# Cross attention over 16 batches: the narrow product before the projection and the queries, the tokens' product before the small ones, Wout loaded in batch 1, another order in the last batch

## The chip, the cores and the metric

The kernel runs on one core of a Trainium2 chip. The metric is the device time of one execution in microseconds, lower is better. All data are float32.

## The reference

For each of 16 batches there are 100 rows of hidden states `x` (640 wide) and 722 context rows (384 wide), of which the last 4 are the tokens `ca` and the first 718 are `enc`. With 8 heads of 80:

```python
query, keyt, valt = x @ Wq, enc @ Wk, enc @ Wv
hs = mha(query, keyt, valt)                          # 100 queries, 718 keys
ca_q1 = einsum('btc,th->bch', ca, Wq_ca)[:, indices] # 100 of 384 rows
ca_hs1 = mha(ca_q1, x, x)                            # 100 queries, 100 keys
ca_hs2 = mha(ca_hs1 @ Wq, ca @ Wk_ca, ca @ Wv_ca)    # 100 queries, 4 keys
out = (hs + ca_hs2) @ Wout + b_out + x
```

`mha` scales by 1/sqrt(80), takes a softmax over the keys and multiplies with the values.

## The kernel before

Everything is laid out once and then one loop runs over the batches `b`. Inside the loop the order of instructions on each engine is the order of the program text (the loop stands under a manual schedule). Tiles come from pools with a fixed number of buffers, and an instruction that writes a tile waits for the last reader of the buffer's former tile. PSUM has three pools of two buffers: `ps2` (pairs of banks), `psk` and `ps1` (single banks).

One turn of the loop does, on TensorE (PE) in this order, with the names that the profile shows:

- `s_ps` (L643), the scores of batch b in three groups, 32 contraction rows at a time in four row groups of the array. ScalarE (ACT) copies them to `st`, VectorE (DVE) takes their running maximum `most`.
- `z_ps` (L842, `softmax2`), 32 small products of the first token softmax `e1` with `y`, in column groups of 32.
- `y_ps` (L780, `second.products`), the tokens' product of batch b + 1: ten matmul passes over the whole array. GpSimd (POOL) makes the first token scores of batch b + 1 from it (`scores1`), which wait for DVE's maximum.
- `v_psA` to `v_psE` (L468) and `k_psA` to `k_psE` (L499), the values of batch b and the keys of batch b + 1, in 15 blocks each after a fast matrix multiplication plan; each block's result is added into `vs` or `kT` by DVE or copied by ACT (L439, L441). `vv.go(n)` and `kk.go(n)` issue the next n blocks; between them stand the steps of the softmax: `top.go` (the maximum over keys, turned with DVE transposes), `subtract(i)` and `exponential(i)` on `st`, and the second token softmax (`scores2`, `softmax3`). `softmax3` ends with `p2t` on DVE, which goes through DRAM (`p_d`, `wide_d`) into `pb`, from which POOL makes `hs2` (`values2`, L918 and L922).
- `kT_ps` (L593), the last chunk of the keys of batch b + 1.
- `o_ps` (L1037, `last.project`), the output projection of a row block of 128 rows that is complete. Row blocks do not line up with batches; it runs in batches 2, 3, 4, 6, 7, 8, 10, 11, 12, 14 and 15. DVE adds it to `xn` (x plus bias), and SyncE (SP) stores it.
- `q_ps` (L569, `queries`), the queries of two batches, in odd batches up to 13.
- `r_ps` (L1385), the narrow product: sums of exponentials and the last 16 values of each head, in column groups of 32. `mine.divide` follows: ACT and DVE invert the sums, SP spreads them through DRAM into `ratio`, and ACT and DVE write the last chunk of `hsT`.
- `a_ps` (L1403), the wide product: the other 64 values of each head, in column groups of 64. `keep` copies it to `hsT`, and `place` on POOL scales it by `ratio` and adds `hs2`.

`wout_sb`, the projection's weights, lies where a weight of the start-up was, and is loaded by ten DMAs that POOL issues in batch 0 (`load_outputs`, L84 and L90).

Batch 15 has no next batch: no `y_ps`, no keys, no queries. It projects 64 rows early (`project_few`, L1065), a block of 128 rows between `r_ps` and `a_ps`, and the last 128 rows after `a_ps`; there `finish` on DVE does what `keep` and `place` do elsewhere.

Of the kernel before, what the change touches and what calls it, by code (L numbers as in the profile page):

```python
# [10 lines left out]
ALU = mybir.AluOpType  # L11
# [142 lines left out]
def kernel(  # L154
# [779 lines left out]
    class Last:  # L934


        def __init__(self, b):
            self.b = b
            self.split = b == B - 1
# [87 lines left out]
        def project(self, chunks=(HC - 1, *range(HC - 1))):  # L1027
            for r, xn in self.xn.items():
                lo, n = OC[r]
                if self.split:  # L1030
                    self.o_ps = [bank(f"o_ps_{r}_{k}") for k in range(2)]
                else:
                    self.o_both = pair(f"o_ps_{r}")
                    self.o_ps = [self.o_both[:, k] for k in range(2)]
                o_ps = self.o_ps
                for c, k in [(c, k) for k in range(2) for c in chunks]:
                    nc.tensor.matmul(  # L1037
                        o_ps[k][:n, : H // 2],
                        hsTs[r][:, c, :n],
                        wout_sb[:, c, k * (H // 2) : (k + 1) * (H // 2)],  # L1040
                        start=(c == chunks[0]),
                        stop=(c == chunks[-1]),
                    )
                o_v = out.rearrange("b s n -> (b s) n")[lo : lo + n]
                if self.split:
                    for k in range(2):
                        cols = slice(k * (H // 2), (k + 1) * (H // 2))
                        nc.vector.tensor_tensor(
                            xn[:n, cols], o_ps[k][:n, : H // 2], xn[:n, cols], ALU.add
                        )  # L1050
                        nc.sync.dma_start(out=o_v[:, cols], in_=xn[:n, cols])
                    continue
                both = xn[:n].rearrange("p (k d) -> p k d", k=2)
                nc.vector.tensor_tensor(
                    both, self.o_both[:n, :, : H // 2], both, ALU.add
                )
                nc.sync.dma_start(out=o_v, in_=xn[:n])
# [155 lines left out]
    for b in range(B):  # L1213
# [5 lines left out]
        def loads():  # L1219

            if b == 0:
                load_outputs(nc.gpsimd.dma_start, wout_sb, wout)
            if b + 2 >= B:
                return None, None
            x_next = xT_at[0] if b % 2 else load_x(p + 1)
            xT_at[0] = x_next
            return Second(b + 2, x_next), load_enc(b + 2)
# [33 lines left out]
        now.softmax2()  # L1261
        if b + 1 < B:
            second.products()
            second.copy()
        seen = larger(2)
# [34 lines left out]
        elif b + 1 < B:  # L1300
# [8 lines left out]
            if b + 2 < B:  # L1309
                m_next = load_m(b + 2)  # L1310
                keys(m_next)
            top.go(3)
# [34 lines left out]
            last.project()  # L1347
        else:
# [5 lines left out]
            last.project_few(len(OC) - 2)  # L1354
            now.scores2()
# [66 lines left out]
    last.project()  # L1422
# [50 lines left out]
```

## Time and profile before

| | |
|---|---|
| timed runs | 941.51, 944.74, 940.45 us; median 941.51 |
| the profiled execution | 942.46 us, its span 940.5 us |
| granted TensorE clock, mean | 0.999 |
| PE busy | 925.5 us, 98% |
| DVE, POOL, ACT busy | 659.0 (70%), 600.7 (64%), 377.4 us (40%) |
| DMA, mean | 74 GB/s |
| share of the chain that ended last | PE 91%, DVE 4%, DMA 2%, issue 1%, POOL 1% |

PE, DVE, ACT and POOL are the engines; PEld is the loading of PE's weights, which overlaps PE. SPq, POOLq and ACTq are the queues that issue DMAs. A float32 matmul shows as two passes, so five matmuls are x10. In the timeline a row is a run of like instructions: start, length from the first start to the modelled end of the last, and then engine, line, operation, out<-in and tile (rows * columns of the array). In the chain of waits the pieces do not overlap, and "issue" is time in which an engine waited for nothing that the profile shows. A row of the waits gives the total, the number of times and the longest. A row of the windows gives the stretch, its length, then busy time and instructions of PE, PEld, DVE, ACT and POOL, the granted clock, the DMA engines' mean busy share and GB/s.

### The profile page before, as it was taken

To read this page: it belongs to the slowest core of one execution; us is meant where nothing else is said; L and a number is where in the kernel's file an instruction comes from. 1 tells how busy PE (TensorE), PEld (TensorE's weight loads), DVE (VectorE), ACT (ScalarE), POOL (GpSimd) and SP (SyncE) were. 2 spreads that over 40 slices of the span, in tenths; PEclk is the share of its full clock that TensorE was granted. 3 is DMA by queue.
4 is the path that set the end of the run, shared out by engine and by line. 5 is a ranking of instruction groups with operands and counts; after the bars stand their busy time and mean duration, and the time that the engine had idled before them with its cause. 6 is when DMAs were issued, how large, how long until landed. Compare 5 with 4: busy or idle time off the path is not lost.

```text
span 940.5 us, 26015 instructions
## 1 busy us (share of the span) xinstructions
PE 925.5 (98%) x11183; PEld 784.4 (83%) x11183; DVE 659.0 (70%) x1102; ACT 377.4 (40%) x649; POOL 600.7 (64%) x616
## 2 busy tenths in 40 slices
PE   9999999999999999999999999999999999999997
PEld 6998879788797888988788888988889788897855
DVE  3359794977929678495955959488692977849592
ACT  1235444434334344543425434344432434443340
POOL 5848699667466774658674575775756668564543
PEclk9999999999999999999999999999999999999999
DMA  8613523051410404132131412205141050402202
GB/s 266 200 39 74 141 64 86 1 144 29 107 43 11 140 9 108 29 87 86 28 94 29 119 40 60 70 8 143 30 108 42 2 144 14 107 26 54 61 23 76
DMA packets 68267, 69.16 MB, mean 74 GB/s; under 512 B 26040, under 2 KB 62072, under 8 KB 68152
## 3 DMA queue, kind: packets, MB, share of 16 engines
q1 hardware_dynamic: 66280, 64.54, 25.7%
q0 software_dynamic: 1008, 1.98, 1.0%
q8 instruction: 88, 1.44, 0.6%
q10 hardware_dynamic: 864, 0.98, 0.3%
q14 instruction: 27, 0.22, 0.1%
HBM read 61.81 MB, written 8.94 MB: 75 GB/s over the span
## 4 chain that ended last, share of the span: by engine, by line
PE 91%; DVE 4%; DMA 2%; issue 1%; POOL 1%; ACT 1%; POOLq 0%; SPq 0%; ACTq 0%; DVEq 0%
PE s_ps L643 12%; PE v_psA L468 10%; PE v_psB L468 8%; PE kT_ps L593 8%; PE k_psA L499 7%; PE q_ps L569 7%; PE a_ps L1403 7%; PE o_ps L1037 6%; PE k_psB L499 6%; PE r_ps L1385 4%; PE v_psC L468 3%; PE k_psC L499 3%; PE y_ps L780 2%; PE v_psD L468 2%; PE v_psE L468 1%; PE v_ps L409 1%
## 5 line engine op out<-in xcount | busy, mean ns | idle before, releaser
L918 POOL TENSOR_TENSOR hs<-pb,vaT 128x500 f32<-128x500 f32 x64 | 79.9, 1258 | 164.7 <-DMA pb<-wide_d 162.2
L815 POOL TENSOR_TENSOR e<-ca,g 100x800 f32<-100x800 f32 x64 | 100.7, 1584 | 68.4 <-DVE most L1245 58.4
L468 PE MATMUL v_psA<-wv_sb,enc 128*120 128x320 f32 x352 | 109.8, 435 | 0.7 <-DVE vs L439 0.6
L534 POOL TENSOR_TENSOR enc<-enc 128x240 f32<-128x240 f32 x135 | 94.2, 708 | 16.9 <-PE q_ps L569 9.8
L643 PE MATMUL s_ps<-qp,kT 32*120 32x100 f32 x3072 | 100.3, 263 | 2.5 <-issue 2.4
L643 PEld LDWEIGHTS s_ps<-qp,kT 32*120 32x120 f32 x3072 | 96.7, 180 | 5.5 <-issue 3.5
L822 POOL TENSOR_TENSOR e<-e,e 100x800 f32<-100x800 f32 x48 | 93.5, 1947 | 3.8
L468 PE MATMUL v_psB<-wv_sb,enc 128*120 128x320 f32 x296 | 91.9, 433 | 0.9 <-DVE vs L439 0.9
L1256 DVE TENSOR_TENSOR most<-st 120x800 f32<-120x800 f32 x16 | 19.5, 1220 | 99.5 <-ACT st L671 99.5
L499 PE MATMUL k_psA<-enc,wk_sb 128*128 128x240 f32 x360 | 87.7, 367 | 0.0
L1245 DVE TENSOR_TENSOR most<-most,st 120x800 f32<-120x800 f32 x64 | 70.6, 1102 | 23.2 <-ACT st L665 22.1
L1233 DVE TENSOR_TENSOR st<-st,over 120x1600 f32<-120x1600 f32 x47 | 86.0, 1830 | 0.0
L468 PEld LDWEIGHTS v_psA<-wv_sb,enc 128*120 128x120 f32 x352 | 63.2, 183 | 23.8 <-DVE vs L439 1.6
L499 PEld LDWEIGHTS k_psA<-enc,wk_sb 128*128 128x128 f32 x360 | 68.4, 190 | 16.6 <-POOL enc L534 0.2
L1241 ACT ACTIVATE st<-st 120x1600 f32<-120x1600 f32 x48 | 73.7, 1538 | 18.8 <-DVE st L1233 17.8
L468 PEld LDWEIGHTS v_psB<-wv_sb,enc 128*120 128x120 f32 x296 | 54.2, 183 | 22.9 <-DVE vs L439 1.4
L499 PE MATMUL k_psB<-enc,wk_sb 128*128 128x240 f32 x300 | 73.0, 366 | 0.0
L922 POOL TENSOR_TENSOR hs<-hs,hs 128x500 f32<-128x500 f32 x48 | 68.4, 1426 | 3.8
L1403 PE MATMUL a_ps<-st,vs 120*64 120x100 f32 (+1 forms) x1536 | 69.5, 250 | 0.0
L569 PE MATMUL q_ps<-xT,wq_sb 128*128 128x200 f32 x400 | 69.1, 333 | 0.0
L1403 PEld LDWEIGHTS a_ps<-st,vs 120*64 120x64 f32 (+1 forms) x1536 | 66.4, 137 | 2.7 <-issue 2.6
L569 PEld LDWEIGHTS q_ps<-xT,wq_sb 128*128 128x128 f32 x400 | 67.9, 190 | 0.6
(167 smaller groups left out, 1830.2 us busy)
## 6 DMA issues: line engine op xcount, KB each, us to landing
pb<-p_d SPq DMA_DIRECT2D x32, 400.0 KB
enc<-in_enct SPq DMA_DIRECT2D x30, 240.0 KB
enc<-in_enct SPq DMA_DIRECT2D x15, 360.0 KB
xT<-in_xt SPq DMA_DIRECT2D x8, 500.0 KB
rest<-in_enct SPq DMA_DIRECT2D x31, 120.0 KB
xn<-in_x SPq DMA_DIRECT2D x11, 320.0 KB
out<-xn SPq DMA_DIRECT2D x11, 320.0 KB
wide_d<-p_d SPq DMA_DIRECT2D x16, 200.0 KB
```

Of the source, the lines that this page charges most:

```text
L468: nc.tensor.matmul(at[0][j][:KN, : H // 2], a_form(self.enc, f)[:, j * KN : (j + 1) * KN], wv_there.get(f, wv_sb[:, W_AT[f]]), start=first ...
L499: nc.tensor.matmul(at[:, i * KT : (i + 1) * KT], wk_sb[:, W_AT[f], i], a_form(self.enc, f), start=(first and i == 0), stop=last, skip_grou ...
L534: nc.gpsimd.tensor_tensor(out, left, right, op)
L569: nc.tensor.matmul(q_ps[:, : 2 * S].rearrange("p (j s) -> p j s", j=2), wq_sb[:, c, n * P : (n + 1) * P], xT[:, :, c, :], start=(c == 0), ...
L593: nc.tensor.matmul(bank[:, i * KT : (i + 1) * KT], weights[c], a_raw(enc, u, c), start=(i == 0 and c == 0), stop=(c == CC - 1), skip_group ...
L643: nc.tensor.matmul(s_ps[bank][:n, 256 * a + lo : 256 * a + lo + rhs.shape[-1]], kT[rows, c, u, j * KN : (j + 1) * KN], rhs, start=bank not ...
L815: first = nc.gpsimd.tensor_tensor(to, self.ca[:, t, :].unsqueeze(1).to_broadcast([S, NH, S]), g[:, :, t].unsqueeze(2).to_broadcast([S, NH, ...
L822: nc.gpsimd.tensor_tensor(e, e, to, ALU.add)
L918: first = nc.gpsimd.tensor_tensor(to, pb[:, :, t], va.to_broadcast([P, HC, S]), ALU.mult)
L1233: return engine.tensor_tensor(st[i], st[i], top.over[:KN].unsqueeze(1).to_broadcast([KN, 2, ROWS]), ALU.subtract,)
L1241: nc.scalar.activation(st[i], st[i], AF.Exp, scale=SCALE)
L1403: nc.tensor.matmul(wides[64 * e : 64 * e + 64, h // 2], slot(i, h, FIRST[e], 64), st[i // 2][: KEYS[i], i % 2, h * S : (h + 1) * S], start ...
```

## The change

Four edits:

- In the loop `r_ps` and `divide` move ahead of the projection and the queries (and POOL's sums for the next context and the exponential of the first token softmax), so that the order on PE is `kT_ps`, `r_ps`, `o_ps`, `q_ps`, `a_ps` instead of `kT_ps`, `o_ps`, `q_ps`, `r_ps`, `a_ps`. SP then stores the projection's rows after the transfers of `ratio` instead of ahead of them.
- `second.products` and `second.copy` move ahead of `softmax2`: `s_ps`, `y_ps`, `z_ps` instead of `s_ps`, `z_ps`, `y_ps`.
- The ten loads of `wout_sb` go from POOL's queue at the end of batch 0 to SP's queue near the start of batch 1, after `load_m`.
- In batch 15 the block of 128 rows is projected in halves of 320 columns, the first after `project_few`, the second after `r_ps`, each with a bank, an add and a store of its own. `softmax3` moves ahead of three blocks of values, `subtract(0)` goes from DVE to POOL, and the seven blocks and two exponentials behind stand in another order.

```diff
-        def project(self, chunks=(HC - 1, *range(HC - 1))):
+        def project(self, halves=(0, 1), apart=False):
             for r, xn in self.xn.items():
...
+                if not apart:
+                    both = pair(f"o_ps_{r}")
+                for k in halves:
+                    cols = slice(k * (H // 2), (k + 1) * (H // 2))
+                    o_ps = psumk(f"o_ps_{r}_{k}") if apart else both[:, k]
+                    for c in (HC - 1, *range(HC - 1)):
+                        nc.tensor.matmul(
+                            o_ps[:n, : H // 2],
+                            hsTs[r][:, c, :n],
+                            wout_sb[:, c, cols],
+                            start=(c == HC - 1),
+                            stop=(c == HC - 2),
+                        )
+                    if apart:
                         nc.vector.tensor_tensor(
-                            xn[:n, cols], o_ps[k][:n, : H // 2], xn[:n, cols], ALU.add
+                            xn[:n, cols], o_ps[:n, : H // 2], xn[:n, cols], ALU.add
                         )
                         nc.sync.dma_start(out=o_v[:, cols], in_=xn[:n, cols])
...
-            if b == 0:
-                load_outputs(nc.gpsimd.dma_start, wout_sb, wout)
...
-        now.softmax2()
         if b + 1 < B:
             second.products()
             second.copy()
+        now.softmax2()
...
                 keys(m_next)
+            if b == 1:
+                load_outputs(nc.sync.dma_start, wout_sb, wout)
             top.go(3)
...
             second.softmax1()
-            last.project()
         else:
...
             last.project_few(len(OC) - 2)
+            last.project((0,), True)
             now.scores2()
             top.go(1)
             vv.go(2)
             top.go()
-            vv.go(3)
             now.softmax3()
-            subtract(1, nc.gpsimd)
+            for i in (0, 1):
+                subtract(i, nc.gpsimd)
             now.values2()
-            vv.go(2)
-            subtract(0)
-            exponential(0)
-            vv.go(2)
-            exponential(1)
+            vv.go(7)
+            for i in (0, 1):
+                exponential(i)
             vv.go(3)
             subtract(2)
             exponential(2)
-        if 0 < b < B - 2:
-            enc_sums(enc_next)
-        if b % 2 and b + 1 < B:
-            xT, tiles = xT_at[0], queries_tiles(p + 1)
-            for n in range(HC):
-                queries(p + 1, xT, tiles, n)
-        if 0 < b < B - 1:
-            second.exponentials1()
-
         rests = psum1(f"r_ps_{b}")[:, : 2 * S].rearrange("p (e q) -> p e q", e=2)
...
         mine.divide(rests)
         if b == B - 1:
+            last.project((1,), True)
+        elif b:
             last.project()
+        if 0 < b < B - 2:
+            enc_sums(enc_next)
+        if b % 2 and b + 1 < B:
+            xT, tiles = xT_at[0], queries_tiles(p + 1)
+            for n in range(HC):
+                queries(p + 1, xT, tiles, n)
+        if 0 < b < B - 1:
+            second.exponentials1()
+
         wides = psum1(f"a_ps_{b}")[:, : 4 * S].rearrange("p (c q) -> p c q", c=4)
...
-    last.project()
+    last.project(apart=True)
```

More of the change, by code (lines that the diff above doesn't have):

```diff
@@ L938, in __init__ @@
             self.b = b
-            self.split = b == B - 1
         def load(self):
@@ L1025, in finish @@
                     nc.vector.tensor_tensor(out, out, self.hs2[:, lo:hi, cols], ALU.add)
-        def project(self, chunks=(HC - 1, *range(HC - 1))):
+        def project(self, halves=(0, 1), apart=False):
             for r, xn in self.xn.items():
                 lo, n = OC[r]
[L1030 to L1043, printed above, removed]
-                o_v = out.rearrange("b s n -> (b s) n")[lo : lo + n]
-                if self.split:
-                    for k in range(2):
-                        cols = slice(k * (H // 2), (k + 1) * (H // 2))
+                o_v = out.rearrange("b s n -> (b s) n")[lo : lo + n]
+                if not apart:
[12 more added lines that the diff above has]
+                    if apart:
@@ L1048, in project @@
                         nc.vector.tensor_tensor(
-                            xn[:n, cols], o_ps[k][:n, : H // 2], xn[:n, cols], ALU.add
+                            xn[:n, cols], o_ps[:n, : H // 2], xn[:n, cols], ALU.add
                         )
                         nc.sync.dma_start(out=o_v[:, cols], in_=xn[:n, cols])
[L1052 to L1056, printed above, removed]
@@ L1057, in project @@
-                nc.sync.dma_start(out=o_v, in_=xn[:n])
+                if not apart:
+                    xn_v = xn[:n].rearrange("p (k d) -> p k d", k=2)
+                    nc.vector.tensor_tensor(
+                        xn_v, both[:n, :, : H // 2], xn_v, ALU.add
+                    )
+                    nc.sync.dma_start(out=o_v, in_=xn[:n])
         def project_few(self, r):
```

## The prediction

> **What bounds the kernel now.** I read the page first, then the waits of PE, then the chain that ended last.
>
> ```profile
> span 940.5 us, 26015 instructions
> PE 925.5 (98%) x11183; PEld 784.4 (83%) x11183; DVE 659.0 (70%) x1102; ACT 377.4 (40%) x649; POOL 600.7 (64%) x616
> ...
> q8 instruction: 88, 1.44, 0.6%
> ```
>
> PE is busy 98% of the span, so only three things can move the time: an idle stretch of PE, the seams between its groups of matmuls, and the ends of the run where PE waits for something else. The profiled execution took 942.46 us with a span of 940.5; the median of the three timed runs is 941.51, so 0.95 below it. I make the sum against 942.46 and carry the difference over.
>
> ```profile
> PE s_ps L643 <- issue: 2.4, 2, 1.9
> ...
> PE z_ps L842 <- issue: 0.9, 2, 0.5
> PE y_ps L780 <- issue: 0.7, 1, 0.7
> ```
>
> These are the waits of PE inside the main loop that name no engine and no DMA: 4.0 us in five places, all in the scores (s_ps), the small products (z_ps) or the tokens' product (y_ps). The chain shows the longest, and milder cases of the same in other batches:
>
> ```profile
> 99.21 3.17 PE s_ps L643 x103
> 102.38 1.89 issue
> 104.27 4.44 PE s_ps L643 x125
> ...
> 158.31 7.65 PE s_ps L643 x236
> ...
> 327.59 7.51 PE s_ps L643 x240
> ...
> 437.46 7.54 PE s_ps L643 x236
> ...
> 499.11 7.28 PE s_ps L643 x240
> ```
>
> An undisturbed scores stage takes 7.28. In batch 1 it took 3.17 + 1.89 + 4.44 = 9.50, so 2.22 too long, of which 1.89 is shown as idle; the other 0.33 lies under the modelled ends of the matmuls. The three stages at 7.65, 7.51 and 7.54 lose another 0.37 + 0.23 + 0.26 = 0.86. My estimate of all such losses is 2.22 for batch 1, 2.1 for the rest of the 4.0 idle, 4 x 0.33 = 1.3 hidden beside it, and 0.86: 6.5 us.
>
> What they wait for, I infer from the page: the instruction queue brought 88 packets, and 2 x 11183 PE instructions over 88 is 254 a packet. The narrow product (r_ps), the wide one (a_ps), s_ps and z_ps stand back to back in the old order and are PE's densest stretch, so a late packet shows there.
>
> The Trainium skill, "Runtime: NRT & Kernel Launch", section "Instruction fetch mechanics", has blocks of 256 instructions and calls the fetch hidden. The block size agrees with the 254; the idle "issue" rows above do not agree with "hidden". By that page nothing is to be had here, and the sum below would come out as that of the first rival.
>
> **The order of PE's groups: what the seams cost.** The change moves r_ps from behind the output projection (o_ps) and the queries (q_ps) to ahead of them, and y_ps from behind z_ps to ahead of it. No matmul is added or dropped in batches 1 to 14. PE's timeline in an old even batch:
>
> ```profile
> 425.02 0.57 PE L593 MATMUL kT_ps<-rest,wk 128*128 128x240 f32 x2
> 425.43 5.55 PE L1037 MATMUL o_ps<-wout_sb,hsT 128*128 128x320 f32 x20
> 430.90 2.28 PE L1385 MATMUL r_ps<-st,vs 120*32 120x100 f32 x96
> 433.12 4.34 PE L1403 MATMUL a_ps<-st,vs 120*64 120x100 f32 x96
> 437.39 1.10 PE L643 MATMUL s_ps<-qp,kT 32*120 32x100 f32 x32
> ...
> 444.44 0.56 PE L643 MATMUL s_ps<-qz,kT 32*120 32x200 f32 x5
> 444.93 0.75 PE L842 MATMUL z_ps<-y,e 100*32 100x33 f32 x64
> 445.61 1.21 PE L780 MATMUL y_ps<-m,xT 128*100 128x96 f32 x10
> 446.65 1.26 PE L468 MATMUL v_psA<-wv_sb,enc 128*120 128x320 f32 x4
> ```
>
> Add start and length of a row and compare with the next start. Between two groups that use the whole array (kT_ps to o_ps, y_ps to v_psA) the next begins 0.16 to 0.17 before the end of the last. Where the tile shape changes (o_ps to r_ps, r_ps to a_ps, a_ps to s_ps, s_ps to z_ps, z_ps to y_ps) it begins only 0.07 before. A change of shape therefore costs about 0.09. The new neighbours are shown at the edges of the run, in batches 0 and 15:
>
> ```profile
> 92.15 0.57 PE L593 MATMUL kT_ps<-rest,wk 128*128 128x240 f32 x2
> 92.65 1.59 PE L1385 MATMUL r_ps<-st,vs 120*32 120x100 f32 x64
> ...
> 900.49 1.34 PE L468 MATMUL v_psA<-wv_sb,enc 128*120 128x320 f32 x4
> ...
> 919.54 0.90 PE L1385 MATMUL r_ps<-st,vs 119*32 119x100 f32 x32 [1.19 <-ACT st L1241]
> 920.37 5.65 PE L1037 MATMUL o_ps<-wout_sb,hsT 128*128 128x320 f32 x20
> 925.95 1.25 PE L1403 MATMUL a_ps<-st,vs 120*64 120x100 f32 x24
> ```
>
> kT_ps to r_ps overlaps by 0.07, r_ps to o_ps by 0.07, o_ps to a_ps by 0.07. And o_ps behind r_ps takes 5.65 instead of 5.55: entering the whole array from small tiles costs another 0.10. v_psA behind a product in small tiles takes 1.34 instead of 1.26, 0.08 more. So:
> - r_ps ahead: the smooth seam into o_ps or q_ps is lost (0.09) and an entry is added (0.10), 0.19 in each of 14 batches: +2.7 us. For batches with only q_ps I take the same, as q_ps uses the whole array too.
> - y_ps ahead: the smooth seam y_ps to v_psA is lost (0.09) and z_ps to v_psA adds an entry (0.08), 0.17 in 15 batches: +2.5 us. s_ps to y_ps is not in the trace; I price it as s_ps to z_ps, and the entry of y_ps is paid in both orders. If it ran smoothly the 2.5 would be about 1.2; nothing reaches below zero.
>
> Together +5.2 us, certain unless the shape rule fails. The Trainium skill says the same in "TensorEngine Tiling (Array Packing)", section "Key Properties": changing the tiling mode drains TensorE. By it the change is a loss wherever it adds a mode change, which it does twice a batch.
>
> **What the order may give back.** With r_ps ahead of a_ps by all of o_ps, q_ps or both (5.55 above, 8.62 below), the dense stretch loses its first 2 x 96 instructions, and y_ps puts 1 us of slow matmuls inside the stretch ahead of z_ps: each wait at z_ps or y_ps was at most 0.7 idle, so I count these as gone. The scores keep their place in the instruction stream, so their packets fall on the same matmuls; what changes there is the other traffic. SP's queue today:
>
> ```profile
> 437.99 0.59 SPq L951 DMA_DIRECT2D xn<-in_x  x1
> 438.63 0.43 SPq L742 DMA_DIRECT2D mb<-m_d  x1
> ...
> 428.63 1.43 DVE L832 TENSOR_TENSOR e<-e,over 100x800 f32<-100x800 f32 x1
> ```
>
> These loads stand behind the ratio loads, which wait for r_ps, so they fell on the first microseconds of the scores (s_ps began at 437.39). With r_ps early, the divide starts when DVE is free of the first softmax, at 428.63 + 1.43 = 430.06, instead of after the end of r_ps at 433.18: 3 us earlier, and about 6 in odd batches. The xn add and its store now queue behind divide on DVE and SP; nothing on PE waits for them before the next scores, 4 us later. So most disturbances of the scores should go. Wout is a case of its own:
>
> ```profile
> 83.70 0.68 POOL L84 DMA_DIRECT2D wout_sb<-in_wout  x1
> ...
> 92.00:108.60 16.60, 14.71 (x436) 13.74 (x434) 9.89 (x20) 7.31 (x13) 7.26 (x10) 1.00 0.78 201
> ```
>
> Its ten issues on POOL's queue, from 83.70, share the DMA engines with batch 0's probability copies, behind which SP issues the next batches' inputs; as I read it, these inputs came late for it and met the stage with the 2.22 loss, where the DMA engines were busy 0.78 of the time. On SP's queue in batch 1 the ten stand behind the mb load and ahead of the p2t stores, which wait for a softmax late in the batch; POOL loses the issues, and its next work waits for the probability copies anyway. By my estimate Wout then lands in the second half of the same scores stage. Bounds are 0 and 2.2 left; I take 0.6, nearer to 0, since only that half is met. The first reader, batch 2's projection, comes a whole batch later. I leave 0.3 for batch 15. Stalls: 0.9 left of 6.5, -5.6 us.
>
> **The last batch.**
>
> ```profile
> 902.32 0.49 DVE xn L1072
> ...
> 906.68 0.79 DVE vs L439 x2
> ...
> 907.56 1.56 DVE vs L439 x2
> ...
> 910.42 0.22 DVE p2t L888
> ...
> 931.10 0.27 DVE spare L1025
> ```
>
> The end hangs on DVE's p2t, the copies of it through DRAM, POOL's products, and DVE at 931.10; the wide product ended only just before (925.95 + 4.34 as above = 930.29). The new order takes four adds into vs out from ahead of p2t: 0.79 + 1.56 = -2.35. It also puts half a projection, ten matmuls or 2.7 us, on PE at 900.49 and its add on DVE after the add at 902.32: that add cannot end before 903.9, and the step after it began at 902.81, so +1.1. Net -1.2. PE loses DVE's adds as they move back and r_ps ends about 1.4 later, but o_ps behind it is halved (-2.8), so a_ps ends near 929 and does not decide. Subtracting st_0 goes to POOL, idle there; the half's store stands on SP ahead of the p2t stores but waits for an add that DVE does before p2t anyway; single banks instead of pairs for the projections change nothing in length. Bounds: -2.4 if the half's add costs nothing, +0.5 if PE comes last.
>
> **Sum.** +5.2 - 5.6 - 1.2 = -1.6 us: 942.46 becomes 940.9, the median 941.5 becomes 939.9.
>
> **Rivals.**
> - Drains unpaid (slower). The packets fall on the same scores matmuls as before, and the loss moves rather than goes. Then +5.2 - 1.2 = +4.0: 945.5, and more with each new stall. It decides if fewer than 4.0 of the 6.5 us go. For it: the seams are sure, the stalls inferred. Against it: the undisturbed 7.28 in many batches. Chance 0.20.
> - More gain. No stall left (0.9), s_ps to y_ps smooth (1.3), and the half's add hidden (1.1): -1.6 - 0.9 - 1.3 - 1.1 = -4.9, so 936.6; a point lower if the estimate of 6.5 is too small by the same. For it: every disturbed scores stage has a transfer on it. Against it: three things at once. Chance 0.22.
> - Wout only changes its place: its 2.22 stays, 1.6 more than forecast: 941.5. Chance 0.07.
> - A new wait in odd batches without projection (1, 5, 9, 13). The fourth query product reuses the bank of r_ps and so waits for divide, which DVE starts after its softmax:
>
> ```profile
> 369.40 8.62 PE L569 MATMUL q_ps<-xT,wq_sb 128*128 128x200 f32 x50
> ...
> 372.59 1.45 DVE L832 TENSOR_TENSOR e<-e,over 100x800 f32<-100x800 f32 x1
> ```
>
> DVE is free at 374.0 and divide needs some 2 us by my estimate, so 376; r_ps would end at 371.7 and the fourth product begin 3/5 of 8.5 later, at 376.8. 0.8 of slack: hidden. If divide takes 2 us more, 1.2 in four batches is about +5, hence 945. Chance 0.05.
>
> **How the numbers follow.** The forecast has 0.46 and a range of its own of 938 to 942 (1.3 of seams, 0.9 of stalls and 1.1 at the end, either way). Half a percent, 4.7 us, is about what a measurement of this kernel can tell from no change: faster means below 936.8, slower above 946.2. Faster: 0.15 of the second rival's 0.22 and 0.04 of the forecast, 0.19. Slower: about half of the first rival's 0.20, as it starts at 945.5, and 0.02 of the last, 0.12. Same: 0.69. The range runs from 935.8, inside the second rival, to 945.8, inside the first; about 0.1 is left out at each end.
>
> **What would show it.** After: kT_ps ends 0.07 into r_ps and o_ps takes 5.65 in every even batch; PE's "issue" waits fall from 4.0 to under 1; scores stages stand at 7.28; p2t lies 1.2 nearer to the start of batch 15. I am wrong if "issue" stays near 4 (first rival), if a wait of q_ps for DVE appears (last), or if seams cost under 3 us in all.

## The result and the profile after

The changed kernel takes 944.73 us (median of 17 runs, 942.88 to 946.43) beside 940.65 for the kernel before (17 runs, 937.53 to 944.74): a ratio of 1.0044, 95% interval 1.0033 to 1.0055. It is 0.4% slower, where 0.2% faster was forecast: within the half percent and the range, but on the other side. The profiled execution took 945.24 us, with a granted clock of 0.996 where it was 0.999 before. It is 2.78 us above the profiled execution of the kernel before (942.46), where the medians are 4.08 apart: the two traces show two thirds of the loss.

The page's first lines and the waits of PE (us in total, times, longest):

```profile
span 943.4 us, 25973 instructions
PE 930.2 (99%) x11183; PEld 783.5 (83%) x11183; DVE 666.3 (71%) x1102; ACT 376.5 (40%) x649; POOL 589.5 (62%) x607
...
PE v_psC L468 <- DVE vs L439: 3.4, 1, 3.4
PE a_ps L1399 <- issue: 1.8, 1, 1.8
PE r_ps L1370 <- ACT st L1235: 1.1, 1, 1.1
```

Two things are to be seen. The "issue" waits of the scores, the small products and the tokens' product are gone, 4.0 us before, and one of 1.8 in the wide product has come. And PE waits 3.4 us for DVE at one place where it did not wait before. That place is in the last batch; PE's timeline there, and then DVE's and POOL's (start, length, work):

```profile
907.02 1.24 PE L468 MATMUL v_psB<-wv_sb,enc 128*120 128x320 f32 x4
911.63 2.49 PE L468 MATMUL v_psC<-wv_sb,enc 128*120 128x320 f32 x4 [3.37 <-DVE vs L439]
913.91 2.34 PE L468 MATMUL v_psA<-wv_sb,enc 128*120 128x320 f32 x4
916.04 2.12 PE L468 MATMUL v_psC<-wv_sb,enc 128*120 128x320 f32 x4
917.99 1.24 PE L468 MATMUL v_psB<-wv_sb,enc 128*120 128x320 f32 x4
...
929.49 4.35 PE L1399 MATMUL a_ps<-st,vs 120*64 120x100 f32 x96
933.76 6.05 PE L1036 MATMUL o_ps<-wout_sb,spare 128*128 128x320 f32 x20
```

```profile
907.62 3.34 DVE L881 TENSOR_TENSOR p_in<-e,sm 100x32 f32<-100x32 f32 x1
910.99 0.21 DVE L888 STREAM_TRANSPOSE p2t<-p_in 128x32 f32<-128x32 f32 x1
911.12 0.85 DVE L439 TENSOR_TENSOR vs<-v_psE,vs 120x320 f32<-120x320 f32 x2
...
907.36 7.08 POOL L1227 TENSOR_TENSOR st<-st,over 120x1600 f32<-120x1600 f32 x2 [11.28 <-DVE sm L879]
```

Read the second fence from its last row. POOL begins its two subtractions at 907.36; the first takes 3.55 of the 7.08 and so ends at 910.91. DVE's multiply into `p_in`, 32 elements a row, begins 0.26 later and ends at 910.96. Its length is what is left of POOL's first subtraction. Only then come `p2t` and DVE's add of `v_psE`, which frees the bank that PE's `v_psC` waits for: the 3.37 us. And when PE goes on, three groups of four matmuls take 2.1 to 2.5 us instead of 1.24. The windows say why (length, then busy time and instructions of PE, PEld, DVE, ACT, POOL, then the granted clock):

```profile
911.63:918.10 6.47, 6.47 (x13) 4.07 (x14) 2.39 (x4) 2.67 (x4) 2.81 (x1) 0.52 0.33 81
918.10:922.50 4.40, 4.40 (x17) 2.48 (x15) 3.12 (x5) 1.74 (x2) 0.19 (x1) 1.00 0.71 164
```

The clock stood at 0.52 for 6.5 us behind the idle stretch.

To see where the time lies I cut each profiled execution in three: up to the start of `m_ps` (start-up), from there to the start of the last batch's scores (loop), and from there to the end of the span (last batch). All points are starts in PE's timeline.

| kernel | `m_ps` | last scores | end | loop | last batch |
|---|---|---|---|---|---|
| before | 21.34 | 885.52 | 940.5 | 864.18 | 54.98 |
| after | 20.91 | 885.34 | 943.4 | 864.43 | 58.06 |

The loop is 0.25 longer and the last batch 3.1.

### The profile page after: what moved, and what is told of

The parts are those of the page before. It is cut to its first block, busy times and chain, and to the rows that moved or that the text cites. A ratio compares the mean times of both kernels' runs of the same rounds, so it can differ in the third digit from the quotient of the medians.

```text
span 943.4 us, 25973 instructions
## 1 busy us (share of the span) xinstructions
PE 930.2 (99%) x11183; PEld 783.5 (83%) x11183; DVE 666.3 (71%) x1102; ACT 376.5 (40%) x649; POOL 589.5 (62%) x607
## 4 chain that ended last, share of the span: by engine, by line
PE 95%; DVE 3%; issue 1%; ACT 1%; DMA 0%; POOL 0%; DVEq 0%; ACTq 0%
PE s_ps L643 12%; PE v_psA L468 10%; PE v_psB L468 8%; PE kT_ps L593 8%; PE k_psA L499 7%; PE a_ps L1399 7%; PE q_ps L569 7%; PE o_ps L1036 7%; PE k_psB L499 6%; PE v_psC L468 4%; PE r_ps L1370 4%; PE k_psC L499 3%; PE y_ps L780 2%; PE v_psD L468 2%; PE v_psE L468 2%; PE v_ps L409 2%
## 5 line engine op out<-in xcount | busy, mean ns | idle before, releaser
L468 PE MATMUL v_psA<-wv_sb,enc 128*120 128x320 f32 x352 | 111.7, 440 | 0.3 <-ACT st L671 0.3
L643 PE MATMUL s_ps<-qp,kT 32*120 32x100 f32 x3072 | 97.5, 263 | 0.0
L643 PEld LDWEIGHTS s_ps<-qp,kT 32*120 32x120 f32 x3072 | 94.7, 180 | 2.1 <-issue 0.2
L1239 DVE TENSOR_TENSOR most<-most,st 120x800 f32<-120x800 f32 x64 | 67.3, 1052 | 21.6 <-ACT st L665 20.5
```

What stands on the lines that cost most here:

```text
L468: nc.tensor.matmul(at[0][j][:KN, : H // 2], a_form(self.enc, f)[:, j * KN : (j + 1) * KN], wv_there.get(f, wv_sb[:, W_AT[f]]), start=first ...
L643: nc.tensor.matmul(s_ps[bank][:n, 256 * a + lo : 256 * a + lo + rhs.shape[-1]], kT[rows, c, u, j * KN : (j + 1) * KN], rhs, start=bank not ...
```

## The experiments

Theory T: the loss is the last batch's, by the chain POOL's subtraction, `p_in`, idle PE, slow clock. Rival: the drains are unpaid, the loop's seams cost 5.2 us and bring nothing. The first four kernels part them. A ratio without a name is to the kernel before, with its 95% interval. Where two changed kernels are compared, each was timed beside the kernel before and mostly not beside the other, so the difference of two ratios is good to some 0.2%, and smaller ones are at the edge of the noise.

**The old last batch in the changed kernel** (`e1_old_tail`): everything that the change does in the branch of batch 15 is undone, the split projection included.

```diff
-            last.project((0,), True)
             now.scores2()
...
+            vv.go(3)
             now.softmax3()
-            for i in (0, 1):
-                subtract(i, nc.gpsimd)
+            subtract(1, nc.gpsimd)
             now.values2()
-            vv.go(7)
-            for i in (0, 1):
-                exponential(i)
+            vv.go(2)
+            subtract(0)
+            exponential(0)
+            vv.go(2)
+            exponential(1)
```

> The changed kernel with the last batch as it was before (adds into vs ahead of p2t, both subtractions where they were, whole projection behind the narrow product); loop order and place of Wout stay as changed. Theory T (the loss is all in the last batch: POOL's first subtraction runs beside DVE's multiply into p_in, which takes 3.34 us there, PE then idles 3.37 us, and its clock is halved for some 6 us): the 3.1 us between the start of the last scores and the end of the span go, the loop's +0.25 stays: about 941 to 941.6, ratio to before 1.000 to 1.001. Rival 'drains unpaid' (the seams cost 5.2 us and are not given back): stays at 944 to 945, ratio 1.0035 to 1.0045.

1.0015 (0.9995 to 1.0034). Last batch 55.14 us, as before; `p_in` 0.91 again. So the new last batch costs the changed kernel 0.29%. What is left, 0.15%, is more than the 0.25 us of the loop, but its interval includes that; in this run the loop took 865.49.

**The new last batch in the kernel before** (`e2_new_tail`): the same edit the other way round, with the new `project`.

```diff
+            last.project((0,), True)
             now.scores2()
...
-            subtract(1, nc.gpsimd)
+            for i in (0, 1):
+                subtract(i, nc.gpsimd)
             now.values2()
...
+            vv.go(7)
```

> The kernel before with the changed last batch alone (half a projection early, first subtraction on POOL, adds into vs behind p2t). Theory T: p_in takes about 3.3 us beside POOL's subtraction and the whole +3.1 us appears without any change of the loop: about 943.7 to 944.2, ratio 1.0033 to 1.0038. Rival 'drains unpaid': the last batch is worth the forecast -1.2 or nothing: 939.5 to 940.7, ratio 0.9988 to 1.000.

1.0029 (1.0013 to 1.0044): the same 0.29% from the other side. DVE and PE:

```profile
908.74 3.34 DVE L881 TENSOR_TENSOR p_in<-e,sm 100x32 f32<-100x32 f32 x1
...
912.75 2.49 PE L468 MATMUL v_psC<-wv_sb,enc 128*120 128x320 f32 x4 [3.37 <-DVE vs L439]
915.03 1.56 PE L468 MATMUL v_psA<-wv_sb,enc 128*120 128x320 f32 x4
916.42 1.24 PE L468 MATMUL v_psC<-wv_sb,enc 128*120 128x320 f32 x4
```

The same 3.34 and 3.37. But the slow clock lasted about half as long here, and the last batch took 56.74: 1.8 us more than before in this trace, not the whole 3.1 that was expected.

**POOL held back** (`e3_hold_pool`): one wait is added to the changed kernel.

```diff
-            nc.vector.transpose(turned, p2_in)
+            self.turned = nc.vector.transpose(turned, p2_in)
...
-            for i in (0, 1):
-                subtract(i, nc.gpsimd)
+            wait_for(subtract(0, nc.gpsimd), now.turned)
+            subtract(1, nc.gpsimd)
```

> The changed kernel, but POOL's first subtraction in the last batch waits until DVE has transposed p2 (p2t), so that POOL is idle while DVE multiplies into p_in. Theory T: p_in takes 0.2 us (as in batches where POOL is idle), p2t is ready near 908.2 instead of 911.2, PE's idle stretch of 3.37 us before v_psC falls under 1, the granted clock stays at full speed through the stage, POOL's products end near 929, span about 938.5 and time 939.7 to 940.3: 4.5 to 5 us below the changed kernel, ratio to before 0.999 to 0.9995. Rival A (p_in is long for another reason, its operands or DVE's own queue): p_in stays near 3.3 us, time stays at 944 to 945, and a later subtraction could add up to 1. Rival B (the half projection and the order itself cost it): p_in falls, but the span does not fall by more than 1 us.

1.0002 (0.9984 to 1.0021), 0.42% or 4 us below the changed kernel; the 0.999 to 0.9995 that was expected lies a little lower, within the interval. DVE, POOL and PE:

```profile
909.62 0.19 DVE L881 TENSOR_TENSOR p_in<-e,sm 100x32 f32<-100x32 f32 x1
...
910.20 7.13 POOL L1227 TENSOR_TENSOR st<-st,over 120x1600 f32<-120x1600 f32 x2 [12.12 <-DVE p2t L888]
...
910.49 1.34 PE L468 MATMUL v_psC<-wv_sb,enc 128*120 128x320 f32 x4 [0.21 <-DVE vs L439]
```

`p_in` falls from 3.34 to 0.19, PE's wait from 3.37 to 0.21, the last batch from 58.06 to 52.15. (The span of 939.5 is one with a late start-up, `m_ps` at 22.89.) Both rivals fall.

**PE kept busy** (`e4_keep_busy`): the wait for DVE stays, and PE multiplies for nothing meanwhile.

```diff
-            vv.go(7)
+            vv.go(3)
+            busy = psumk("busy")
+            for _ in range(6):
+                nc.tensor.matmul(
+                    busy[:, : H // 2], ident, wout_sb[:, 0, : H // 2], start=True, stop=True
+                )
+            vv.go(4)
```

> The changed kernel with six extra products of 128x128 by 128x320 into an unused PSUM bank, issued in the last batch just ahead of the first v_psC, so that PE works through the 3.37 us in which it waits for DVE; the rest is unchanged and the extra result is thrown away. Theory T (the slow products after that wait are the clock, and the clock follows the idle time): v_psC still starts near 911.6, but the three groups of four take about 1.25 us each instead of 2.49, 2.34 and 2.12, the granted clock stays near 1.0 there, r_ps starts near 919.4 instead of 922.55; the end is then set by POOL's products (932.2) and gains 1 to 2 us: 942.7 to 943.7. Rival (the products are slow for their operands or for traffic beside them): the groups stay at 2.1 to 2.5 us and the time at 944.7 or above, by as much as the extra work delays.

1.0025 (1.0011 to 1.0039), 0.19% below the changed kernel. PE's timeline, and a window behind the extra work:

```profile
911.05 3.39 PE L1362 MATMUL busy<-wout_sb,ident 128*128 128x320 f32 x12
914.59 1.34 PE L468 MATMUL v_psC<-wv_sb,enc 128*120 128x320 f32 x4
915.92 1.34 PE L468 MATMUL v_psA<-wv_sb,enc 128*120 128x320 f32 x4
...
914.59:922.70 8.11, 8.11 (x28) 4.79 (x28) 5.53 (x9) 4.41 (x5) 2.81 (x1) 1.00 0.47 118
```

`p_in` still takes 3.35, but the clock stays at 1.00 and the groups take 1.34. The slow matmuls were the clock, and the clock followed the idle stretch. The last batch takes 55.41: of the 5.9 us that the held POOL saves, 2.65 are the clock's. It is the trace that shows this. In the times 0.19% is at the edge of the noise, and this profiled execution is no shorter in all (span 943.7), because its loop lost 2.7 us more, most of it in batch 1 (below, at Wout).

**The same wait in the kernel before** (`e13_before_hold`), whose last batch has one subtraction on POOL:

```diff
-            subtract(1, nc.gpsimd)
+            wait_for(subtract(1, nc.gpsimd), now.turned)
```

> The kernel before, in whose last batch POOL's only subtraction there (of st_1) waits until DVE has transposed p2. Theory T (DVE's multiply into p_in cannot go on while POOL's subtraction runs): p_in takes 0.2 us instead of 0.91, p2t ends 0.7 earlier after the start of the last scores (24.4 instead of 25.1), and the end, which hangs on p2t, with it: -0.7, ratio 0.9993. Rival (0.91 is what this multiply takes there for its own reasons): p_in stays at 0.9, ratio 1.000.

0.9984 (0.9966 to 1.0003), not resolved from 0.9993 or from 1. The trace decides:

```profile
909.44 0.19 DVE L881 TENSOR_TENSOR p_in<-e,sm 100x32 f32<-100x32 f32 x1
...
910.02 5.01 POOL L1233 TENSOR_TENSOR st<-st,over 120x1600 f32<-120x1600 f32 x1 [9.85 <-DVE p2t L888]
```

0.19 instead of 0.91: the 0.91 in the kernel before was already the rest of POOL's instruction (906.76 + 3.58 = 910.34; `p_in` ended at 909.48 + 0.91 = 910.39). And POOL's subtraction, which now meets DVE's own, grows from 3.58 to 5.01: the blocking goes both ways. The last batch took 53.44, 1.5 less than before; 0.7 of that is the earlier `p2t`, and 0.9 a quicker way of it through DRAM, which this edit does not explain.

Next the loop, part by part. Here the theory (S) is that each moved product takes away the stalls near it, and the rival is again that the drains are unpaid.

**The narrow product ahead, alone** (`e5_r_only`): the first edit of the change, in the kernel before.

```diff
             second.softmax1()
-            last.project()
         else:
...
-        if 0 < b < B - 2:
-            enc_sums(enc_next)
-        if b % 2 and b + 1 < B:
...
         mine.divide(rests)
-        if b == B - 1:
+        if b:
             last.project()
+        if 0 < b < B - 2:
+            enc_sums(enc_next)
+        if b % 2 and b + 1 < B:
...
```

> The kernel before with one part of the change alone: in batches 1 to 14 the narrow product (r_ps) and divide stand ahead of the output projection and the queries. Seams, by both theories: kT_ps to r_ps 0.30 from the last start to the next (0.20 before), projection of twenty 5.58 instead of 5.48, q_ps of fifty 8.655 instead of 8.551; +0.19 in each of 14 batches, +2.7. Theory S (the 'issue' stalls of the scores come from loads behind the ratio, which now go out earlier): scores from batch 2 on stand at 7.28, -1.8, while the scores of batch 1 (9.50) and the stalls of z_ps (some 2.3 in all) stay: net +0.9, ratio to before 1.001. Rival 'drains unpaid': the scores' stalls stay too, net +2.7, ratio 1.0029.

0.9977 (0.9966 to 0.9989): better than both. The seams are there, the scores stand at 7.28 from batch 2 on, and z_ps loses 0.78 where it lost 2.3. The scores of batch 1, which were expected to stay at 9.50, took 8.38. The loop took 863.26, 0.9 less than before. PE's waits show a new one:

```profile
PE q_ps L569 <- DVE hsT L983: 1.0, 1, 1.0
PE s_ps L643 <- issue: 0.8, 1, 0.8
...
PE z_ps L842 <- issue: 0.3, 1, 0.3
```

That is the prediction's last rival, once, in batch 1. The last batch was 53.41, 1.6 less than before, in that one execution; 1.3 of it is a quicker way of `p2t` through DRAM.

**The tokens' product ahead, alone** (`e6_y_only`): the second edit.

```diff
-        now.softmax2()
         if b + 1 < B:
             second.products()
             second.copy()
+        now.softmax2()
```

> The kernel before with another part alone: in each batch the tokens' product (y_ps) stands ahead of the small ones (z_ps). Seams, by both theories: y_ps 1.135 instead of 1.042 to the next start and v_psA entered 0.08 later, +0.17 in 15 batches, +2.5. Theory S: the stalls of z_ps and y_ps (2.3 and some 0.9) go, z_ps at 0.678 in every batch, the stalls of the scores (4 us in all) stay: net -0.7, ratio to before 0.999 to 0.9995. Rival 'drains unpaid': the late instructions are late at y_ps or at the first v or k product instead, net +2.5, ratio 1.0027.

1.0001 (0.9988 to 1.0014): the stalls of z_ps and y_ps are gone from the loop and the seams have come, nothing is won. The scores of batch 1 lost 4.3 us in this profile where they lost 2.2 before (why, below).

**Wout in batch 1, alone** (`e12_wout_only`): the third edit. Theory V, which stands in the next texts, says that the gains of the parts add up, and that what the changed kernel lacks of their sum is the price of Wout's new place.

```diff
-            if b == 0:
-                load_outputs(nc.gpsimd.dma_start, wout_sb, wout)
...
                 keys(m_next)
+            if b == 1:
+                load_outputs(nc.sync.dma_start, wout_sb, wout)
             top.go(3)
```

> The kernel before with Wout's ten loads alone moved, from POOL's queue in batch 0 to SP's queue in batch 1 behind the load of mb. Theory V: +3 to +3.5 us, as the sum of the parts demands, ratio 1.003 to 1.0037, and the trace shows new stalls of PE in batch 1. Rival 'Wout only changes its place': the stall of batch 1 (s_ps 2.2 too long) stays about as long or moves into a_ps, ratio 0.9985 to 1.001.

0.9999 (0.9979 to 1.0018). Theory V falls; Wout changes the place of the stall of batch 1, from the scores (2.2) to the wide product (1.7, and 0.3 in the scores):

```profile
PE a_ps L1403 <- issue: 1.5, 1, 1.5
```

The loop took 862.38 in this trace, 1.8 less than before, as other stalls were shorter too, and the last batch 56.49, 1.5 more, with a wait of `v_psA` for DVE of 1.8 us; the times show neither.

**The tokens early** (`e9_x_early`): the changed kernel with POOL held back, and one load of the burst ahead of that stall moved away.

```diff
-            x_next = xT_at[0] if b % 2 else load_x(p + 1)
+            x_next = xT_at[0] if b % 2 or b == 0 else load_x(p + 1)
...
+            xT_at[0] = load_x(1)
             now.softmax3()
```

> The changed kernel with POOL's first subtraction held back until p2 is transposed, and batch 0's load of the next pair's tokens (xT) issued ahead of the probability stores instead of behind them, so that it no longer joins the loads of enc and rest at 91 to 99 us. Theory W (the 1.9 us stall in the wide product of batch 1 is an instruction fetch behind that burst of loads, and Wout, which is issued at 104 us there, has no part in it): the wide product of batch 1 falls from 6.16 to 4.3 to 5.0, 1 to 1.9 us below the kernel with the wait alone, ratio to before 0.998 to 0.9992. Rival (the stall does not follow these loads): it stays at 5.8 or more, ratio 1.000.

1.0002 (0.9987 to 1.0017), a miss: the load was issued at 38.63 instead of 90.9, and the wide product of batch 1 still took 6.21. In the scores behind it another 2.5 us were lost.

**The new last batch with the wait, in the kernel before** (`e8_new_tail_hold`): as the second kernel, and

```diff
-            for i in (0, 1):
-                subtract(i, nc.gpsimd)
+            wait_for(subtract(0, nc.gpsimd), now.turned)
+            subtract(1, nc.gpsimd)
```

> The kernel before, whole loop as it was, with the changed last batch, in which POOL's first subtraction waits until DVE has transposed p2. Theory T (the new last batch is good once POOL keeps out of DVE's multiply): from the start of the last scores to the end of the span 52.2 us, as in the changed kernel with the same wait (before 55.0, changed 58.1), p_in 0.2 us, no idle stretch of PE over 1 us before v_psC: -2.8 us, ratio to before 0.9965 to 0.998. Rival (the gain of that wait hangs on the new loop order): 55 us, ratio 1.000.

0.9981 (0.9969 to 0.9993). The last batch took 52.19, as with the new loop. So the new last batch is worth 0.2%, and without the wait it costs 0.3%.

**All but Wout, with the wait** (`e10_old_wout`) and **the narrow product and the last batch, with the wait** (`e11_r_tail_hold`) differ only in the place of the tokens' product. The first is the changed kernel with the wait and

```diff
+            if b == 0:
+                load_outputs(nc.gpsimd.dma_start, wout_sb, wout)
...
-            if b == 1:
-                load_outputs(nc.sync.dma_start, wout_sb, wout)
```

and the second has besides

```diff
+        now.softmax2()
         if b + 1 < B:
             second.products()
             second.copy()
-        now.softmax2()
```

> The changed kernel with POOL's first subtraction held back until p2 is transposed, and Wout loaded as before: on POOL's queue in batch 0. Against the kernel with the wait alone (ratio 1.0002) only the place of Wout differs. Theory V (the parts add up, and what is missing from their sum is Wout's new place): narrow product ahead -2.1 (measured), tokens' product ahead +0.1 (measured), last batch with the wait -1.7 (measured), sum -3.7: ratio to before 0.996 to 0.997. Rival 'lottery' (the stall at the first blocks after batch 0 differs from kernel to kernel by 1 to 5 us, whatever Wout does): the ratio stays at 0.9985 to 1.0005.

0.9997 (0.9981 to 1.0013): as the same kernel with Wout in its new place (1.0002), and in the range of the rival 'lottery'.

> The kernel before with the narrow product ahead in batches 1 to 14 and with the new last batch and its wait; tokens' product and Wout as before. The sum of the two parts as measured is -2.1 and -1.7: ratio 0.996, the fastest of all kernels here, by 938.5. Rival: 1.3 of the 2.1 us of the narrow product alone came from a shorter way of p2t through DRAM in the last batch (12.2 us before, 10.9 there, from p2t to POOL's first product), by chance, and it is not to be had twice: 0.9975.

0.9958 (0.9943 to 0.9972): the two parts add up to the digit (-0.23% and -0.19%). Theory V asked for the same of the kernel with the tokens' product ahead as well; that one is 0.39% slower. So the missing piece is not Wout but the tokens' product, which alone cost nothing. The loops say 865.76 against 863.32, +2.44.

**The tokens' product put back in the changed kernel**, with the wait (`e14_y_back_hold`) and without (`e15_y_back`):

```diff
+        now.softmax2()
         if b + 1 < B:
             second.products()
             second.copy()
-        now.softmax2()
```

> The changed kernel with POOL's first subtraction held back until p2 is transposed and with the tokens' product (y_ps) back behind the small ones (z_ps). Theory Y (the early narrow product alone already takes the stalls away, so the tokens' product ahead only pays its seams, 2.5 us, for some 0.5 us of stalls): 2 to 3.7 us below the same kernel with y_ps ahead (ratio 1.0002), ratio to before 0.9963 to 0.998, and z_ps stalls of under 1 us in all in the trace. Rival (the two moves together are what keeps the scores at 7.28): stalls of 2 us or more come back in z_ps and s_ps, ratio 0.9995 or above.

> The changed kernel with the tokens' product back behind the small ones and nothing else undone, so with POOL's subtraction beside DVE's multiply into p_in. Theory Y: 2 to 3.7 us below the changed kernel (1.0044): ratio to before 1.0005 to 1.0023, with the idle stretch of 3.4 us before v_psC still there. Rival: as the changed kernel, 1.004 or above.

0.9957 (0.9937 to 0.9977) and 1.0020 (0.9999 to 1.0041): 0.45% and 0.24% below the same kernels with the product ahead; the second difference alone would be at the edge of the noise. The first is as fast as the best above, with a span of 935.6; the second still has the fault in its last batch:

```profile
PE v_psC L468 <- DVE vs L439: 3.4, 1, 3.4
```

## Why the prediction was wrong

**The last batch: the step that failed.** The prediction had "Net -1.2" and, beside it, "Subtracting st_0 goes to POOL, idle there". POOL was idle, but DVE was not free of it. The kernel before had the price in two rows that were not read, 0.91 us for 32 elements a row beside POOL's subtraction:

```profile
906.76 3.58 POOL L1233 TENSOR_TENSOR st<-st,over 120x1600 f32<-120x1600 f32 x1 [6.56 <-DVE over L736]
...
909.48 0.91 DVE L881 TENSOR_TENSOR p_in<-e,sm 100x32 f32<-100x32 f32 x1
```

It stood in the loop as well: over the sixteen batches of that kernel the same multiply takes 0.19 to 1.37 us, and in thirteen of them it ends 0.05 us after an instruction of POOL's.

So a term of +2.4 (3.34 instead of 0.91) was put at nothing. With it `p2t` ended 25.9 us after the start of the last scores where it was 25.1 before: 0.8 later and not 1.2 earlier. The path was wrong as well. The prediction let the end hang on `p2t` and POOL's products and said that `a_ps` "ends near 929 and does not decide". In the changed kernel `a_ps` ended at 929.49 + 4.35 = 933.84, 48.5 after the start of the scores where 929 would have been 43.5, and PE, held up by DVE's late add and then by its clock, came last. The prediction priced that case at +0.5.

The measured cost is +3.1 between the two traces and +0.29%, 2.7 us, in two pairs of kernels. Single traces of a last batch spread: the old one took 53.41 to 56.49 in the five kernels that have it unchanged, the new one 56.74 to 58.06 in three. With POOL held back the same order takes 52.07 to 52.60 in the traces of six kernels, whatever their loop, 2.4 to 2.9 less than the kernel before, and `p2t` ends 2.4 earlier after the start of the scores than before (22.7 against 25.1): the gain that the prediction sought was there, twice its size, 0.7 of it because even the old multiply waited for POOL. The Trainium skill, "SBUF — State Buffer", section "SBUF: two separate sides", calls the port pair of DVE and GpSimd an exclusive lock, held for a whole instruction, where DVE has two SBUF inputs and GpSimd reads SBUF, with the later one fully blocked. The trace agrees (3.34 against 0.19, ending 0.05 after POOL); that rule spoke against this change and was not weighed.

**The clock**, which the prediction did not look at, nearly doubled the loss: 3.37 us of idle time, then 6.5 us at 0.52, which cost 2.65 by `e4_keep_busy`. The Trainium skill, "TensorE: Matmul & The Clock Gate", "Part 1: The HAM clock gate", halves the rate after an idle window of some 3.4 us and gives it back after as long a busy one. The 3.37 us and the halving agree; the slow stretch was 6.5 us here and about half of that in the kernel before with the new last batch. But less idle time was enough elsewhere, as the point on Wout shows.

**The seams, +5.2: right.** An even batch of the changed kernel:

```profile
423.37 0.57 PE L593 MATMUL kT_ps<-rest,wk 128*128 128x240 f32 x2
423.87 2.28 PE L1370 MATMUL r_ps<-st,vs 120*32 120x100 f32 x96
426.08 5.65 PE L1036 MATMUL o_ps<-wout_sb,hsT 128*128 128x320 f32 x20
431.66 4.35 PE L1399 MATMUL a_ps<-st,vs 120*64 120x100 f32 x96
...
442.75 0.54 PE L643 MATMUL s_ps<-qz,kT 32*120 32x200 f32 x8
443.21 1.21 PE L780 MATMUL y_ps<-m,xT 128*100 128x96 f32 x10
444.35 0.75 PE L842 MATMUL z_ps<-y,e 100*32 100x33 f32 x64
445.02 1.34 PE L468 MATMUL v_psA<-wv_sb,enc 128*120 128x320 f32 x4
```

Each of these overlaps its follower by only 0.07 or 0.08, o_ps takes 5.65 and v_psA 1.34, as forecast, s_ps to y_ps included.

**The stalls, -5.6: right in kind, 1.3 too large, wrong in who earns them.** By the starts of PE's groups, the scores and the two products behind them lost 6.3 us in batches 1 to 14 before (the estimate was 6.5), and what is left is 2.0, in the wide product of batch 1: -4.3. Seams and stalls together were forecast at -0.4 and the loop shows +0.25; a wait of PE for DVE of 0.6 in batch 1 went too.

That these waits are late packets of instructions, which the prediction inferred, the traces bear out. In the kernel before, the instruction queue (q8) starts a packet of 1.2 us at 101.67, and the wait of 1.89 us ends 2.6 us after that start, at 104.27; in the changed one a packet starts at 97.40, and the wait of 1.76 ends 2.5 later. The sixteen traces have 35 such waits of 0.3 us or more in the loop, 0.33 to 2.70 long. Every one of them ends 2.2 to 3.3 us after a packet has started and 1.2 to 1.7 after it has landed, while packets lie 10.7 us apart on average (88 in 940.5). What made them late is another question.

Where the prediction erred is in the credit that it gave the tokens' product for the stalls of z_ps and y_ps. The narrow product alone takes most of them away. Its `ratio` loads and those behind them do move off the scores: in an even batch `mb` was issued at 438.63, 1.2 us into the scores, and with the narrow product ahead at 434.40, 1.7 us ahead of them. That this is the cause is argued, not shown; the one run that moves a load by itself (`e9_x_early`) did not shorten its stall. What the tokens' product then adds is its 2.5 us of seams for 0.4 us of stalls: +2.44, +2.35 and, in the pair without the wait, +1.52 in three pairs of traces, 0.24 to 0.45% in three pairs of times. Alone it still had stalls to take away, and came out at nothing. The times ask for somewhat more than the traces (2.3 to 4.2 us against 1.5 to 2.4); with some 2 us of noise on each difference, whether there is a rest at all is open.

**Wout only changes its place: the rival that held**, at 0.07. It priced 1.6 more than forecast; the stall of batch 1 was 2.0 in the wide product instead of 2.2 in the scores, while the scores that Wout then falls on, where the forecast left 0.6, took an undisturbed 7.27. Its reason in the prediction was wrong, though. The changed kernel, its chain and SP's queue:

```profile
98.16 1.76 issue
...
93.67 1.39 SPq L259 DMA_DIRECT2D rest<-in_enct  x2
...
103.71 0.62 SPq L84 DMA_DIRECT2D wout_sb<-in_wout  x1
```

Wout is issued 4 us after the stall is over. What comes just ahead are the next batch's inputs, which are issued some 5 us earlier once Wout is out of their way, and the stall now meets the wide product instead of the scores. That these loads cause it is not shown: taking one of them away did not help (`e9_x_early`), and over all sixteen kernels this stall cost between 1.1 and 5.3 us. Part of that spread is the clock again. The kernel with the idle PE kept busy has the longest stall of the wide product:

```profile
101.32 2.27 PE L1405 MATMUL a_ps<-st,vs 119*64 119x100 f32 x24 [2.17 <-issue]
...
102.00:104.00 2.00, 2.00 (x28) 1.76 (x28) 0.20 (x1) 0.36 (x1) 1.92 (x2) 0.50 0.08 20
```

After 2.17 us of idle time the clock stood at 0.50, and the wide product took 7.68 in all. The same followed 2.29 and 2.70 us in two kernels whose scores lost 4.3 and 4.7 (`e6_y_only`, `e8_new_tail_hold`), and 2.13 us in `e13_before_hold`; after 1.76 and 1.89 us, in the changed kernel and the one before, it stayed at 1.00. So in these traces a stall of 2 us is near a cliff, and kernels with nearly the same code fell on either side of it. What holds the packet up is not settled.

**A new wait of q_ps**: real, 1.0 us (forecast 1.2), in one batch of four, and only with Wout in batch 0. In the kernel before POOL's products of batch 0 begin at 101.98, in the changed one at 95.26:

```profile
101.98 2.02 POOL L918 TENSOR_TENSOR hs<-pb,vaT 128x500 f32<-128x500 f32 x2 [9.03 <-DMA pb<-wide_d]
```

```profile
95.26 2.02 POOL L918 TENSOR_TENSOR hs<-pb,vaT 128x500 f32<-128x500 f32 x2 [8.50 <-DMA pb<-wide_d]
```

Batch 1's first work on POOL waits for them, and so the softmax of batch 1 on DVE, ahead of divide, comes later. With Wout in its new place that wait is gone, which may be why the move costs nothing in all.

**Drains unpaid**: its 945.5 is near the measured 944.73, by another mechanism. Its test, "issue" near 4, did not come true; nor did the forecast's own, under 1 (1.8).

**The sum as measured**, in percent of the time before: narrow product -0.23, tokens' product behind it +0.24 to +0.45, Wout 0, last batch +0.29; together +0.30 to +0.51, where the changed kernel has +0.44. The two good parts with one wait have -0.42, with or without Wout's move.

## What to carry to other kernels

Before giving an idle engine work, look at what the neighbours do at that time and read their odd rows: an instruction whose length changes several times over with what another engine does, 0.19 to 1.37 us here, shows a price that the move can multiply. When two edits remove the same stalls, the second pays its own cost for nothing, so measure each alone and on top of the other. And a wait of PE of 2 to 3 us can cost nearly twice its length; where it can't be removed, a few matmuls that nobody needs were cheaper here, by 2.65 us in the trace.

## What the runs showed of the hardware

- A multiply of 100x32 with two SBUF operands takes 0.19 us on DVE, and 0.91 to 3.35 us when POOL is inside a 120x1600 subtraction: it ends 0.05 to 0.06 us after POOL does. In the loop of the kernel before it waits in the same way for shorter instructions of POOL's. POOL's subtraction in turn takes 3.55 to 3.58 us, and 5.01 where DVE has a 120x1600 subtraction of its own beside it.
- After 3.37 us without a matmul the granted clock was 0.52 for 6.5 us in one trace and 0.55 for 3.3 us in another, and after 2.13 and 2.17 us it fell to 0.50 too; after 1.89 us it stayed at 1.00, and with matmuls in the gap of 3.4 us as well.
- PE's waits in the loop that name no engine and no DMA of 0.3 us or more, 35 in sixteen traces, all ended 1.2 to 1.7 us after a packet of instructions had landed, whatever their length. They moved with the order of the program and the place of Wout's loads, and in batch 1 cost 1.1 to 5.3 us in kernels whose code up to there is nearly the same.
